# Projection matmuls of a graph layer's prologue issued ahead of their evictions, in PSUM banks of their own

## The chip, the cores and the metric

The kernel runs on one core of a Trainium2 chip. The metric is the device time of one execution in microseconds, as the median of several runs. A profiled execution has a time of its own, and the profile's "span" is the stretch of it that the trace covers.

## The reference, cut to what matters

The kernel computes one layer of a graph transformer for 6250 nodes of 256 features and 206,250 edges sorted by their target. Three parts follow each other: an attention over the edges, a linear attention over all nodes whose result is added to it, and a layer of eight experts.

```python
xn = _layernorm(x, axis=-1)
x = x + gnn(xn, edges, Wq, bq, Wk, bk, Wv, bv, Wo, bo) + linear_attention(xn, w_qkv, w_out, b_out)
x = x + experts(_layernorm(x, axis=-1), gate_w, gate_b, w1, b1, w2, b2)

# gnn: r is the source of an edge, c its target; 8 heads of 32
q = (feats @ Wq.T + bq); k = (feats @ Wk.T + bk); v = (feats @ Wv.T + bv)
sim = einsum('hed,hed->eh', q[:, c, :], k[:, r, :]) * scale
p = exp(sim - segment_max(sim, c)[c])
attn = p / segment_sum(p, c)[c]
agg = segment_sum(attn * v[:, r, :], c)
return agg @ Wo.T + bo
```

What the change touches is the first line of the attention: the layer norm of x and its products with the three weight matrices, which give the rows that the edges later gather.

## The kernel before

**Tiling.** The nodes are cut into NB = 49 blocks of P = 128 rows (the last one partly filled). D is 256, so a block's keys and values are a 128x512 tile (2 * D columns), its queries a 128x256 tile. Rows are float32 throughout.

**The prologue** writes two tables in DRAM that the rest of the kernel gathers from. `kv_tab` holds a row of keys and values for each node, `q_tab` a row of queries. It has two loops over the 49 blocks, one after the other.

The mean over features is taken out of the weights (`less_mean`, L219), so a block's matmul works on raw x, and the inverse standard deviation `rstd` is applied in the eviction. A key/value block is therefore: two matmuls over the two halves of D (L519, which the trace shows as four records, as it does for each pair of float32 matmuls) from a transposed copy of x, `xTs[k]`; one VectorE instruction (L530) that multiplies by rstd, adds the bias and writes the row buffer `kv`; one store on SyncE's queue (L533).

**x is loaded in groups** of GX = 4 blocks by `load_x` (L368): once in rows (`xg`, L383, two buffers), which ScalarE sums (`stat_sum`, L409) and squares (`stat_square`, L416) to get rstd, and once transposed (`xT`, L199, three buffers), for the matmuls. The first three groups are issued from SyncE's queue, later ones from ScalarE's own queue, where a load that has to wait for a free buffer holds up the ScalarE instructions behind it. A buffer of xT is free when the four blocks of the group that had it are through TensorE.

**Ranking of the nodes by degree** runs between the blocks of the first loop. `index_step(b)` (L501), called at the end of each block, starts gathers of pieces of the sorted edge list by GpSimd (`row_gathers`, L477; seven blocks to a set), turns them into the start of each node's edges on VectorE (`in_rows`, L488 to L492), and from block 19 on advances a generator, `rank_group` (L266), by one step a block. Its steps: two small matmuls (L271, L272), a one-hot tile (L285), six counting steps of two matmuls (L296, L298) and four VectorE instructions (L308 to L316), then three steps with VectorE one-hot tiles (`lo` L332, one buffer; `hi` L337; `rhs` L344) and up to seven matmuls each (L348).

**PSUM.** [...] The pool `bps` is a ring of five banks which `bank()` (L208) hands out in program order to whatever asks: the blocks' matmuls, the ranks' matmuls, and later all other work of the layer. The pool `qps` has three tiles of one bank each (`qc`, `pr` and `pa` of the attention loop); it exists from the start, and the prologue has no use for it.

**Order.** Each engine works through its instructions in the order of the program, and the program's order is written by hand (a manual schedule). In the first loop a block is: its two matmuls, the statistics that are due, the eviction, the store, `index_step(b)`. So the matmuls of `index_step(b)` stand between those of block b and block b+1 in TensorE's order, and the eviction of block b+1 stands behind VectorE's part of `index_step(b)`. TensorE and VectorE wait for each other by semaphores, where a tile is not ready or a buffer isn't free yet.

**Between the loops** GpSimd issues `gather_to` for the first unit of the attention: 37 gathers of 128 key/value rows each (L602, 256 KB each) into the ring `kvp` of eleven buffers. They wait for the whole of kv_tab.

**The second loop** is the same for queries: two matmuls of 256 columns a block (L616), the eviction (L620) into a row buffer `kv` of the same pool, three buffers in all, and the store to q_tab (L623); xT is loaded a second time, from ScalarE's queue. After it GpSimd gathers the query rows of the first two units (`queries`, L580), which wait for the whole of q_tab, and the attention loop begins (`units`, L1311), with the linear attention and the experts spread between its steps as background work.

Of the kernel before, what the change touches and what calls it, by code (L numbers as in the profile page):

```python
# [9 lines left out]
F32 = mybir.dt.float32  # L10
# [3 lines left out]
ALU = mybir.AluOpType  # L14
AX = mybir.AxisListType
PSUM = bass.MemoryType.PSUM
DRAM = bass.MemoryType.DRAM

P = 128
# [5 lines left out]
W = 5  # L25
# [43 lines left out]
def gps_layer(  # L69
# [34 lines left out]
    nc = tc.nc  # L104
    N, D = x.shape
    E = n_edges
    NB = -(-N // P)
# [5 lines left out]
    DC = D // P  # L113
# [18 lines left out]
    def bcast_row(ap, n, parts=P):  # L132
        return bass.AP(tensor=ap.tensor, offset=ap.offset, ap=[[0, parts], [1, n]])

    dram = ctx.enter_context(tc.tile_pool(name="dram", bufs=1, space=DRAM))
    kv_tab = dram.tile([NB * P, 2 * D], F32, name="kv_tab")
# [15 lines left out]
    with tc.manual_schedule():  # L152
# [15 lines left out]
        ident = keep.tile([P, P], F32, name="ident")  # L168
# [19 lines left out]
        rstd = keep.tile([P, NB], F32, name="rstd")  # L188
# [8 lines left out]
        def x_transposed(to, b, n=1, queue=nc.sync):  # L197

            queue.dma_start(to, xT_all[:, b * DC * P : (b + n) * DC * P])  # L199

        mctx = ExitStack()
        kvp = mctx.enter_context(tc.tile_pool(name="kvp", bufs=RING))
        cp3 = mctx.enter_context(tc.tile_pool(name="c3", bufs=3))
        cp2 = mctx.enter_context(tc.tile_pool(name="c2", bufs=2))
        qps = mctx.enter_context(tc.tile_pool(name="qps", bufs=1, space=PSUM))
        bps = mctx.enter_context(tc.tile_pool(name="bps", bufs=5, space=PSUM))

        def bank(shape):  # L208

            t = bps.tile([P, 512], F32, name="bank")  # L210
            n = math.prod(shape)
            v = t[:, :n]
            if len(shape) == 2:
                v = v.rearrange("p (a b) -> p a b", a=shape[0])
            if len(shape) == 3:
                v = v.rearrange("p (a b c) -> p a b c", a=shape[0], b=shape[1])
            return v
# [36 lines left out]
        def rank_consts(pool):  # L254
            t = {}
            t["ones_b"] = pool.tile([P, P], BF16, name="ones_b")
            nc.vector.memset(t["ones_b"], 1.0)
            t["back_b"] = pool.tile([P, P], BF16, name="back_b")
            nc.vector.tensor_scalar(t["back_b"], after, -1.0, None, op0=ALU.add)
            t["next_p"] = pool.tile([P, P], F32, name="next_p")  # L260
            nc.vector.tensor_scalar(t["next_p"], diff, -1.0, None, op0=ALU.is_equal)
            t["next_b"] = pool.tile([P, P], F32, name="next_b")
            nc.vector.tensor_scalar(t["next_b"], diff, float(P - 1), None, op0=ALU.is_equal)
            return t
# [94 lines left out]
        with ExitStack() as actx:  # L359
            ap1 = actx.enter_context(tc.tile_pool(name="a1", bufs=1))  # L360
            ap2 = actx.enter_context(tc.tile_pool(name="a2", bufs=2))
            ap3 = actx.enter_context(tc.tile_pool(name="a3", bufs=3))

            GX = 4
            NGX = -(-NB // GX)
            xgs, xTs = {}, {}

            def load_x(k, rows_too=True, queue=nc.scalar):  # L368

                if k >= NGX:  # L370
                    return
                b0 = k * GX
                n = min(GX, NB - b0)
                if rows_too:
                    xg = ap2.tile([P, GX, D], F32, name="xg")
                    xgs[k] = xg
                    full = n
                    if b0 + n == NB:
                        full = n - 1
                        nc.vector.memset(xg[:, full, :], 0.0)  # L380
                        queue.dma_start(xg[:tail, full, :], x[(NB - 1) * P : N, :])
                    if full:
                        queue.dma_start(  # L383
                            xg[:, :full, :], x[b0 * P : (b0 + full) * P, :].rearrange("(t p) d -> p t d", p=P)
                        )
                xT = ap3.tile([P, GX, DC, P], F32, name="xT")
                xTs[k] = xT
                x_transposed(xT[:, :n].rearrange("p t c q -> p (t c q)"), b0, n, queue)
# [4 lines left out]
            wn = ap1.tile([P, DC, 3 * D], F32, name="wn")  # L393
            for c in range(DC):
                nc.sync.dma_start(wn[:, c, : 2 * D], w_node[c * P : (c + 1) * P, : 2 * D])
            load_x(0, queue=nc.sync)
            bn = ap1.tile([P, 3 * D], F32, name="bn")
            nc.sync.dma_start(bn, bcast_row(b_node, 3 * D))
            load_x(1, queue=nc.sync)
            for c in range(DC):  # L400
                nc.sync.dma_start(wn[:, c, 2 * D :], w_node[c * P : (c + 1) * P, 2 * D : 3 * D])
            load_x(2, queue=nc.sync)
            rc = rank_consts(ap1)
            sums = ap1.tile([P, 2, NB], F32, name="sums")

# [5 lines left out]
            def stat_square(k):  # L411
                g = slice(k * GX, min(NB, (k + 1) * GX))
                nc.vector.tensor_scalar(sums[:, 0, g], sums[:, 0, g], -1.0 / D, None, op0=ALU.mult)
                for b in range(g.start, g.stop):
                    junk = ap1.tile([P, D], F32, name="junk")
                    nc.scalar.activation(  # L416
                        junk, xgs[k][:, b % GX, :], AF.Square, bias=sums[:, 0, b : b + 1],
                        accum_out=sums[:, 1, b : b + 1],
                    )
                nc.scalar.activation(rstd[:, g], sums[:, 1, g], AF.Sqrt, bias=eps, scale=1.0 / D)  # L420

            def stat_end(k):
                g = slice(k * GX, min(NB, (k + 1) * GX))
                nc.vector.reciprocal(rstd[:, g], rstd[:, g])
# [76 lines left out]
            def index_step(b):  # L501
# [9 lines left out]
                if b >= 8 + 5 * (need0 - 1) + 1:  # L511
                    next(ranks, None)

            stat_end(0)
            for b in range(NB):
                k = b // GX
                pkv = bank((2 * D,))
                for c in range(DC):
                    nc.tensor.matmul(  # L519
                        pkv, xTs[k][:, b % GX, c, :], wn[:, c, : 2 * D], start=(c == 0), stop=(c == DC - 1)  # L520
                    )
                if b % GX == 0 and k + 1 < NGX:
                    stat_square(k + 1)
                if b % GX == GX - 1 and k + 1 < NGX:
                    stat_end(k + 1)
                    load_x(k + 3)
                    if k + 2 < NGX:
                        stat_sum(k + 2)
                kv = ap3.tile([P, 2 * D], F32, name="kv")
                nc.vector.scalar_tensor_tensor(  # L530
                    kv, pkv, rstd[:, b : b + 1], bn[:, : 2 * D], op0=ALU.mult, op1=ALU.add
                )
                nc.sync.dma_start(kv_tab[b * P : (b + 1) * P, :], kv)  # L533
                index_step(b)
            load_x(0, False)
            load_x(1, False)
# [72 lines left out]
            sources(1)  # L609
            gather_to(len(units[0][5]))  # L610
            less_mean(wn[:, :, 2 * D :], D)
            for b in range(NB):
                k = b // GX
                pq = bank((D,))
                for c in range(DC):
                    nc.tensor.matmul(  # L616
                        pq, xTs[k][:, b % GX, c, :], wn[:, c, 2 * D :], start=(c == 0), stop=(c == DC - 1)
                    )
                q = ap3.tile([P, 2 * D], F32, name="kv")[:, :D]
                nc.vector.scalar_tensor_tensor(  # L620
                    q, pq, rstd[:, b : b + 1], bn[:, 2 * D :], op0=ALU.mult, op1=ALU.add
                )
                nc.sync.dma_start(q_tab[b * P : (b + 1) * P, :], q)  # L623
                if b % GX == GX - 1:
                    load_x(k + 3, False)
            queries(0)
            queries(1)

# [3 lines left out]
            nc.vector.tensor_reduce(bad[:, 0:1], down, AX.X, ALU.max)  # L632


        bctx = ExitStack()
        mp1 = bctx.enter_context(tc.tile_pool(name="m1", bufs=1))
        mp2 = bctx.enter_context(tc.tile_pool(name="m2", bufs=2))
# [636 lines left out]
        def weigh(v, c):  # L1274

            j0, j1 = v["chunks"][c]
            m = j1 - j0
            kv = kv_of.pop((v["u"], c))
            if c == 0:
                v["pa"] = qps.tile([P, D], F32, name="pa")  # L1280
            s0, s1 = v["s0"], v["s1"]
            vals = kv[:, :m, D:].rearrange("p j (h d) -> p j h d", d=GD)
            nc.vector.tensor_tensor(  # L1283
                vals, vals, v["pr"][:, j0 - s0 : j1 - s0, :, None].to_broadcast([P, m, GH, GD]), ALU.mult
            )
            for j in range(m):
                nc.tensor.matmul(v["pa"], ident, kv[:, j, D:], start=(j0 + j == s0), stop=(j0 + j == s1 - 1))  # L1287

        def complete(v):

# [18 lines left out]
        v = None  # L1309
        queries_of(0)  # L1310
        for u, (b, part, n_p, s0, s1, chunks) in enumerate(units):  # L1311
# [7 lines left out]
            for c in range(max(len(chunks), n_v)):  # L1319
# [5 lines left out]
                if c < len(chunks):  # L1325
                    gather_to(at + 1 + LEAD)
                    j0, j1 = chunks[c]
# [34 lines left out]
            v = new  # L1362
        for c in range(len(v["chunks"])):
            background(pace[-1] * W)
            weigh(v, c)
# [552 lines left out]
```

## Time and profile before

| What | Value |
|---|---|
| median of 3 runs | 3119.5 us (3118.4 to 3120.74) |
| the profiled execution's own time | 3534.2 us |
| its span | 3532.3 us |
| mean granted clock of TensorE | 0.812 |
| busy: TensorE matmul, VectorE, GpSimd, ScalarE | 66%, 57%, 54%, 18% of the span |
| DMA | 730.28 MB, mean 207 GB/s |
| evictions of keys and values (L530), first to last | 18.46 to 155.61 us |
| evictions of queries (L620), first to last | 158.12 to 245.20 us |
| first gather of query rows (L580) | 248.25 us |

The page and the answers of the trace give an instruction's start in us from the start of the span, its duration, its engine and line, the tiles it writes and reads, and in square brackets how long the engine had been idle before it and what ended that. "PE" is TensorE's matmul, "PEld" its weight load, "DVE" VectorE, "ACT" ScalarE, "POOL" GpSimd, "SPq" and "ACTq" the queues on which SyncE and ScalarE issue DMAs. "issue" is idle time in which the profile shows nothing that was waited for, "remote" one whose releaser it can't name. A list of waits has the waiting engine and line, what it waited for, the total, the number of times and the longest. The profiled execution is longer than an execution without the profiler, by 414.7 us here.

### The profile page before, as it was taken

To read this page: it belongs to the slowest core of one execution; us is meant where nothing else is said; L and a number is where in the kernel's file an instruction comes from. 1 tells how busy PE (TensorE), PEld (TensorE's weight loads), DVE (VectorE), ACT (ScalarE), POOL (GpSimd) and SP (SyncE) were. 2 spreads that over 40 slices of the span, in tenths; PEclk is the share of its full clock that TensorE was granted. 3 is DMA by queue.
4 is the path that set the end of the run, shared out by engine and by line. 5 is a ranking of instruction groups with operands and counts; after the bars stand their busy time and mean duration, and the time that the engine had idled before them with its cause. 6 is when DMAs were issued, how large, how long until landed. Compare 5 with 4: busy or idle time off the path is not lost.

```text
span 3532.3 us, 29535 instructions
## 1 busy us (share of the span) xinstructions
PE 2337.7 (66%) x9086; PEld 1777.0 (50%) x9086; DVE 2023.5 (57%) x2723; ACT 633.9 (18%) x1802; POOL 1920.0 (54%) x2114
## 2 busy tenths in 40 slices
PE   7844457775767643764688887743664988866395
PEld 3433335443444432553576676622543877755394
DVE  4438677776767756676565654555673655545200
ACT  4200013322323200220111111110210111111142
POOL 4243656665666656656665665566546665552101
PEclk8876678888888876896798898866876999887697
DMA  6563956655655655775777776565756887664584
GB/s 215 197 205 103 332 156 182 181 173 168 181 172 176 185 160 167 240 218 176 254 253 241 241 247 230 183 195 176 234 162 215 287 271 255 237 201 139 199 321 141
DMA packets 291643, 730.28 MB, mean 207 GB/s; under 512 B 46838, under 2 KB 152020, under 8 KB 278164
## 3 DMA queue, kind: packets, MB, share of 16 engines
q0 software_dynamic: 149744, 477.83, 44.4%
q1 hardware_dynamic: 133560, 234.37, 18.9%
q10 hardware_dynamic: 8172, 16.10, 1.5%
q8 instruction: 75, 1.23, 0.1%
q14 instruction: 92, 0.75, 0.1%
HBM read 654.47 MB, written 73.64 MB: 206 GB/s over the span
## 4 chain that ended last, share of the span: by engine, by line
PE 38%; issue 20%; DVE 15%; POOL 12%; another core or an unknown queue 6%; DMA 6%; ACT 2%; DVEq 0%; SPq 0%; POOLq 0%; ACTq 0%
PE pa L1287 13%; POOL kvg L602 10%; PE bank L1145 8%; PE bank L1162 8%; DVE kvg L1329 3%; DVE sim L1330 3%; DVE kvg L1283 3%; PE bank L709 2%; DMA kvg<-kv_tab,idx 2%; PE bank L519 2%; PE bank L866 1%; PE bank L1166 1%; PE bank L746 1%; DMA q_tab<-kv 1%
## 5 line engine op out<-in xcount | busy, mean ns | idle before, releaser
L602 POOL DMA_INDIRECT kvg<-kv_tab,idx x1715 | 1624.9, 947 | 900.7 <-issue 466.4
L1287 PE MATMUL pa<-kvg,ident 128*128 128x256 f32 x3430 | 1026.8, 454 | 646.8 <-issue 413.7
L1287 PEld LDWEIGHTS pa<-kvg,ident 128*128 128x128 f32 x3430 | 765.3, 229 | 893.2 <-issue 493.9
L1329 DVE TENSOR_TENSOR kvg<-kvg,qc 128x1280 f32<-128x1280 f32 (+1 forms) x366 | 512.3, 1400 | 334.6 <-DMA kvg<-kv_tab,idx 248.0
L1330 DVE TENSOR_REDUCE sim<-kvg 128x40 f32<-128x1280 f32 (+1 forms) x366 | 513.2, 1402 | 12.6
L1283 DVE TENSOR_TENSOR kvg<-kvg,pr 128x1280 f32<-128x1280 f32 (+1 forms) x366 | 509.5, 1393 | 0.0
L1162 PE MATMUL bank<-wt,hTe 128*128 128x256 f32 x1056 | 269.2, 396 | 44.4 <-issue 43.6
L1145 PE MATMUL bank<-xTe,wt 128*128 128x256 f32 x1056 | 271.0, 405 | 33.8 <-issue 30.3
L1145 PEld LDWEIGHTS bank<-xTe,wt 128*128 128x128 f32 x1056 | 214.3, 204 | 79.1 <-issue 45.6
L1162 PEld LDWEIGHTS bank<-wt,hTe 128*128 128x128 f32 x1056 | 207.2, 199 | 85.0 <-issue 57.2
L1303 DVE TENSOR_TENSOR ag<-pa,s 128x256 f32<-128x256 f32 x46 | 19.5, 423 | 349.8 <-PE pa L1287 242.8
L709 PE MATMUL bank<-wm,xTm 128*128 128x512 f32 x392 | 193.2, 637 | 2.5 <-issue 2.4
L801 POOL DMA_INDIRECT agg_tab<-ag,node_ri x49 | 48.5, 989 | 248.1 <-DVE ag L1303 214.2
L1226 DVE TENSOR_TENSOR res<-bank,row_b 128x256 f32<-128x256 f32 x49 | 20.6, 421 | 270.4 <-ACT bank L1222 222.3
L1151 ACT ACTIVATE hTe<-bank,wt 128x256 f32<-128x256 f32 x264 | 108.0, 474 | 374.6 <-PE bank L1145 134.5
L1205 POOL DMA_INDIRECT row_a<-ybuf,row_from x49 | 46.6, 951 | 199.3 <-issue 190.7
L746 PE MATMUL bank<-ck,cv 128*128 128x128 f32 x392 | 75.6, 340 | 97.7 <-ACT ck L738 82.0
L718 ACT ACTIVATE sq<-bank 128x512 f32<-128x512 f32 x98 | 57.0, 595 | 420.5 <-PE pa L1287 157.5
L746 PEld LDWEIGHTS bank<-ck,cv 128*128 128x128 f32 x392 | 68.2, 241 | 113.4 <-ACT ck L738 90.1
L1168 ACT COPY res<-bank 128x256 f32<-128x256 f32 x85 | 31.6, 372 | 503.1 <-issue 230.5
L709 PEld LDWEIGHTS bank<-wm,xTm 128*128 128x128 f32 x392 | 78.9, 212 | 83.8 <-issue 83.5
L726 DVE TENSOR_REDUCE rv<-sq 128x16 f32<-128x1024 f32 x49 | 59.5, 1214 | 103.2 <-ACT sq L718 71.2
(254 smaller groups left out, 2258.7 us busy)
## 6 DMA issues: line engine op xcount, KB each, us to landing
wt<-in_w_rows_dram SPq DMA_DIRECT2D x33, 1152.0 KB
wt<-in_w_rows_dram SPq DMA_DIRECT2D x33, 1028.0 KB
kvg<-kv_tab,idx POOLq DMA_INDIRECT x1715
kvg<-in_w_rows_dram SPq DMA_DIRECT2D x19, 1152.0 KB
kvg<-in_w_rows_dram SPq DMA_DIRECT2D x19, 1028.0 KB
kv_tab<-kv SPq DMA_DIRECT2D x49, 256.0 KB
in<-xbuf SPq DMA_DIRECT2D x85, 128.0 KB
ybuf<-res SPq DMA_DIRECT2D x85, 128.0 KB
```

The source lines that it names most:

```text
L519: nc.tensor.matmul(pkv, xTs[k][:, b % GX, c, :], wn[:, c, : 2 * D], start=(c == 0), stop=(c == DC - 1))
L602: nc.gpsimd.indirect_dma_start(out=kv[:, j - j0, :], out_offset=None, in_=kv_tab[:, :], in_offset=bass.IndirectOffsetOnAxis(ap=idx_of[b][: ...
L709: nc.tensor.matmul(pm, xT_of[b][:, c, :], wmf[:, c, s * MI : (s + 1) * MI], start=(c == 0), stop=(c == DC - 1),)
L726: nc.vector.tensor_reduce(rv, sqs[b], AX.X, ALU.add)
L746: nc.tensor.matmul(dots[:, hp, :], cvs[b][:, h], ckf[:, h], start=(b == 0 and hp == 0), stop=(b == NB - 1 and hp == HP - 1), skip_group_ch ...
L1145: nc.tensor.matmul(ph[:, k, :], w[:, c, f * P : (f + 1) * P], T[t]["xT"][:, c, :size], start=(k == 0 and c == 0), stop=(k == 1 and c == DC ...
L1151: nc.scalar.activation(T[t]["hT"][:, f, :size], ph[:, k, :], AF.Relu, bias=w1_t[:, V1 + f : V1 + f + 1])
L1162: nc.tensor.matmul(py, T[t]["hT"][:, f, k * P : (k + 1) * P], w[:, f, :], start=(f == 0), stop=False)
L1283: nc.vector.tensor_tensor(vals, vals, v["pr"][:, j0 - s0 : j1 - s0, :, None].to_broadcast([P, m, GH, GD]), ALU.mult)
L1287: nc.tensor.matmul(v["pa"], ident, kv[:, j, D:], start=(j0 + j == s0), stop=(j0 + j == s1 - 1))
L1329: nc.vector.tensor_tensor(keys, keys, qc[:, None, :].to_broadcast([P, j1 - j0, D]), ALU.mult)
L1330: nc.vector.tensor_reduce(sim[:, j0 - s0 : j1 - s0, :], keys.rearrange("p j (h d) -> p j h d", d=GD), AX.X, ALU.add)
```

## The change

The first loop issues the matmuls of a block two blocks ahead of its eviction, in a pool `aps` of three banks of its own; the second loop three blocks ahead. The pool takes the three banks of `qps`, which is opened only after the prologue. Row buffers are six instead of three. The rows of x go to buffers of the gather ring `kvp` instead of two of their own. All loads of x are issued on SyncE's queue, in the first loop after the store of the group's last block, in the second after the store of the group's first. In the call of `weigh` only a line break differs.

```diff
-        qps = mctx.enter_context(tc.tile_pool(name="qps", bufs=1, space=PSUM))
         bps = mctx.enter_context(tc.tile_pool(name="bps", bufs=5, space=PSUM))
...
             ap3 = actx.enter_context(tc.tile_pool(name="a3", bufs=3))
+            ap6 = actx.enter_context(tc.tile_pool(name="a6", bufs=6))
+            aps = actx.enter_context(tc.tile_pool(name="aps", bufs=3, space=PSUM))
...
-            def load_x(k, rows_too=True, queue=nc.scalar):
+            def load_x(k, rows_too=True, queue=nc.sync):
...
-                    xg = ap2.tile([P, GX, D], F32, name="xg")
+                    xg = kvp.tile([P, W, 2 * D], F32, name="kvg")[:, :GX, :D]
...
+            pkvs = {}
+
+            def keys_values(b):
+
+                if b >= NB:
+                    return
+                pkvs[b] = aps.tile([P, 2 * D], F32, name="pkv")
+                for c in range(DC):
+                    nc.tensor.matmul(
+                        pkvs[b], xTs[b // GX][:, b % GX, c, :], wn[:, c, : 2 * D], start=(c == 0), stop=(c == DC - 1)
+                    )
+
             stat_end(0)
+            keys_values(0)
+            keys_values(1)
             for b in range(NB):
                 k = b // GX
-                pkv = bank((2 * D,))
-                for c in range(DC):
-                    nc.tensor.matmul(
-                        pkv, xTs[k][:, b % GX, c, :], wn[:, c, : 2 * D], start=(c == 0), stop=(c == DC - 1)
-                    )
                 if b % GX == 0 and k + 1 < NGX:
                     stat_square(k + 1)
                 if b % GX == GX - 1 and k + 1 < NGX:
                     stat_end(k + 1)
+                kv = ap6.tile([P, 2 * D], F32, name="kv")
+                nc.vector.scalar_tensor_tensor(
+                    kv, pkvs.pop(b), rstd[:, b : b + 1], bn[:, : 2 * D], op0=ALU.mult, op1=ALU.add
+                )
+                nc.sync.dma_start(kv_tab[b * P : (b + 1) * P, :], kv)
+                if b % GX == GX - 1 and k + 1 < NGX:
                     load_x(k + 3)
                     if k + 2 < NGX:
                         stat_sum(k + 2)
-                kv = ap3.tile([P, 2 * D], F32, name="kv")
-                nc.vector.scalar_tensor_tensor(
-                    kv, pkv, rstd[:, b : b + 1], bn[:, : 2 * D], op0=ALU.mult, op1=ALU.add
-                )
-                nc.sync.dma_start(kv_tab[b * P : (b + 1) * P, :], kv)
+                keys_values(b + 2)
                 index_step(b)
             load_x(0, False)
             load_x(1, False)
...
-            for b in range(NB):
-                k = b // GX
-                pq = bank((D,))
+            pqs = {}
+
+            def query_rows(b):
+                if b >= NB:
+                    return
+                pqs[b] = aps.tile([P, 2 * D], F32, name="pkv")[:, :D]
                 for c in range(DC):
                     nc.tensor.matmul(
-                        pq, xTs[k][:, b % GX, c, :], wn[:, c, 2 * D :], start=(c == 0), stop=(c == DC - 1)
-                    )
-                q = ap3.tile([P, 2 * D], F32, name="kv")[:, :D]
+                        pqs[b], xTs[b // GX][:, b % GX, c, :], wn[:, c, 2 * D :], start=(c == 0), stop=(c == DC - 1)
+                    )
+
+            for b in range(3):
+                query_rows(b)
+            for b in range(NB):
+                q = ap6.tile([P, 2 * D], F32, name="kv")[:, :D]
                 nc.vector.scalar_tensor_tensor(
-                    q, pq, rstd[:, b : b + 1], bn[:, 2 * D :], op0=ALU.mult, op1=ALU.add
+                    q, pqs.pop(b), rstd[:, b : b + 1], bn[:, 2 * D :], op0=ALU.mult, op1=ALU.add
                 )
                 nc.sync.dma_start(q_tab[b * P : (b + 1) * P, :], q)
-                if b % GX == GX - 1:
-                    load_x(k + 3, False)
+                query_rows(b + 3)
+                if b % GX == 0 and b:
+                    load_x(b // GX + 2, False)
             queries(0)
             queries(1)
...
+        qps = mctx.enter_context(tc.tile_pool(name="qps", bufs=1, space=PSUM))
```

More of the change, by code (lines that the diff above doesn't have):

```diff
@@ L395, in gps_layer @@
                 nc.sync.dma_start(wn[:, c, : 2 * D], w_node[c * P : (c + 1) * P, : 2 * D])
-            load_x(0, queue=nc.sync)
+            load_x(0)
             bn = ap1.tile([P, 3 * D], F32, name="bn")
             nc.sync.dma_start(bn, bcast_row(b_node, 3 * D))
-            load_x(1, queue=nc.sync)
+            load_x(1)
             for c in range(DC):
                 nc.sync.dma_start(wn[:, c, 2 * D :], w_node[c * P : (c + 1) * P, 2 * D : 3 * D])
-            load_x(2, queue=nc.sync)
+            load_x(2)
             rc = rank_consts(ap1)
@@ L1286, in weigh @@
             for j in range(m):
-                nc.tensor.matmul(v["pa"], ident, kv[:, j, D:], start=(j0 + j == s0), stop=(j0 + j == s1 - 1))
+                nc.tensor.matmul(
+                    v["pa"], ident, kv[:, j, D:], start=(j0 + j == s0), stop=(j0 + j == s1 - 1),
+                )
         def complete(v):
```

## The prediction

> **What bounds the kernel now.** I read the page first, then the chain of waits, then waits and timeline of the first 250 us, since the edit touches nothing else. TensorE is busy 66% of the span, VectorE 57%, GpSimd 54%: no engine is full, and shares of the whole span say little of this stage. All later work hangs on one event, the first gather of query rows (L580), which needs every row of the query table in DRAM:
>
> ```profile
> 207.41 0.95 POOL L602 DMA_INDIRECT kvg<-kv_tab,idx  x1 [0.30 <-issue]
> 248.25 0.94 POOL L580 DMA_INDIRECT qs<-q_tab,node_ri  x1 [39.90 <-DMA q_tab<-kv]
> ```
>
> GpSimd had its 37 key/value gathers out at 208.4 and then stood idle 39.9 us for the last query row. So the prologue is one chain: keys and values of 49 blocks (evictions from 18.46 to 155.61), then queries (158.12 to 245.20). A microsecond taken from it moves the attention loop by a microsecond.
>
> Where does the first stage lose time? Waits between 13 and 157 us (engine, line, what it waited for; total, times, longest):
>
> ```profile
> ACT junk L409 <- PE bank L519: 43.7, 4, 25.0
> DVE kv L530 <- PE bank L519: 27.5, 14, 6.4
> PEld bank L519 <- DVE kv L530: 15.2, 11, 7.2
> PEld bank L348 <- DVE rhs L344: 14.1, 3, 5.4
> DVE kv L530 <- DMA kv_tab<-kv: 9.9, 6, 3.0
> DVE kv L530 <- remote: 7.6, 1, 7.6
> ```
>
> VectorE waits for TensorE and TensorE for VectorE: each holds what the other needs next. The timeline of TensorE and of VectorE shows it in the last three ranking steps:
>
> ```profile
> 98.94 3.25 PE L348 MATMUL bank<-rhs,lo 128*128 128x60 f32 x14 [4.58 <-DVE rhs L344]
> 101.97 3.14 PE L519 MATMUL bank<-wn,xT 128*128 128x512 f32 x4
> ...
> 105.15 0.75 DVE L530 SCALAR_TENSOR_TENSOR kv<-bank,rstd,bn 128x512 f32<-128x512 f32 x1 [6.19 <-PE bank L519]
> 115.45 0.75 DVE L530 SCALAR_TENSOR_TENSOR kv<-bank,rstd,bn 128x512 f32<-128x512 f32 x1 [6.21 <-issue]
> 124.40 0.75 DVE L530 SCALAR_TENSOR_TENSOR kv<-bank,rstd,bn 128x512 f32<-128x512 f32 x1 [6.44 <-PE bank L519]
> ```
>
> The ranking matmuls (L348) wait for VectorE's one-hot tiles, the next block's L519 matmuls stand behind them in TensorE's order, and the eviction waits for those: some 10 us a block. Outside ranking TensorE alone sets the pace: the chain has one piece from 120.83, 34.75 us long, "PE bank L519 x76", 1.72 us a block. In the query stage:
>
> ```profile
> DVE kv L620 <- remote: 26.8, 4, 10.7
> DVE kv L620 <- DMA q_tab<-kv: 23.5, 13, 3.4
> PEld bank L616 <- DVE kv L620: 12.2, 6, 5.6
> DVE kv L620 <- PE bank L616: 6.3, 4, 2.2
> ```
>
> Three row buffers are too few: evictions come in bursts of three and wait for a store to land. Behind the word "remote" stand stalls that no edit touches: block 11 is evicted at 50.16 though TensorE had run four blocks past it by 44.5. The profiled execution took 3534.2 us (span 3532.3), 414.7 more than the median of 3119.5. I read these stalls as part of that excess and count no gain from them; a rival takes the other view.
>
> **What the Trainium skill says.** "Perfetto Trace Analysis", Matmuls, says to rotate independent matmul groups through PSUM banks so that evictions overlap the next matmuls; the trace agrees where only L519 uses the five banks (1.72 us a block without a gap), and not where ranking takes two banks a step. "TensorE: Matmul & The Clock Gate", the HAM clock gate, says that TensorE falls to half clock after an idle window of about 3.4 us; here L519 passes stand 0.43 us apart at clock 1.00 and 0.85 apart after the long idle at 51. "DMA: Bandwidth & Descriptors", Issuing engines are not separate DMA queues, says that another issuing engine saves only the issue time; I use it for the moved loads, and no run shows it yet.
>
> **The change part by part.**
> Matmul count, evictions (0.75 and 0.48 us) and stores are unchanged; what changes is order and buffers.
>
> (1) Keys and values two blocks ahead in three banks. Blocks 0 to 19: L519 passes run at 1.72 us a block from 19.18, so block 20's matmuls would end at 19.18+19x1.72=51.9. The ranks need the third set of row gathers, whose issue GpSimd ends at 48.0 at 1.25 us each; with landing (2 us, as the stall's end at 50.1 suggests) and 1.4 us of L488 to L492 I put the eviction of block 20 at 53.5. Before it is at 69.99. Of these 16.5 us about 10 are the stall (TensorE idle 6.4 us to 50.97, then two blocks at half clock, 3.4): counted gain 6.5. Blocks 20 to 30: before 124.40-69.99=54.4 us. With matmuls ready, VectorE's own work bounds it: block 20: 0.75+1.95=2.7; six counting steps of 2.29 (80.48 to 82.77, eviction and L308 to L316): 13.7; row counting at block 23: 1.45; block 27: 3.8. Then the single buffer lo (L332) makes two steps of 3.25 (L348) plus 2.05 (lo, hi, rhs): 10.6. That is 32 up to the eviction of block 30; with 4 for hand-overs between the engines, 36. TensorE's share, ten blocks of 1.72 and 9.3 of L348, fits beside it. Gain 18. Blocks 31 to 48: banks allow two blocks ready, so 16x1.72+1=28.5 against 31.2: gain 2.7. Sum 27. Where the stall of the eviction goes, lo's single buffer is late next. I take 24, because TensorE may run steps at half clock after its idle gaps and because DMA must carry more: two stages of 128x512 rows, x and x transposed need 512 KB a block, 305 GB/s at 1.72 us; the trace shows up to 387 in a 3 us window, so it fits with little to spare. Bounds 12 to 30.
>
> (2) x through SyncE. In the first stage ScalarE's 43.7 us are cover, not cost: later it is ready in time (after the 25 us wait block 32 is evicted 1.1 us late, and TensorE never stops). Gain 0, bounds -2 to +2. On SyncE's queue each pair of loads, 1 MB, now stands ahead of the next stores: about 3 us at 340 GB/s. Six row buffers give 6x1.72=10.3 us from one use of a buffer to the next, enough for 3 us plus the 5 us that the last store took to land (156.39 to 161.3). The load waits for matmuls whose eviction is already behind it in SyncE's order: no new wait; xg in the gather ring waits for nothing. Three query loads are worse off: ScalarE issued the first at 150.21, ahead of the last evictions; on SyncE it stands behind the store of block 48. 512 KB at 340 GB/s is 1.5 us, with issue and landing about 4, before the first query matmul may start (before: 1.3 after the last eviction started). Cost 4, bounds 2 to 6; the 1.5 MB, 4.5 us, move with it.
>
> (3) Queries three ahead, six buffers. Between 163 and 188, DMA is full (0.94 to 1.03 of its time, 312 to 382 GB/s) at 1.9 us a block (eleven blocks from 164.95 to 185.69): buffers can't help; 0. After the gathers 28 blocks take 214.4 to 245.2, 1.10 each; L616 in one piece (9.76 us for 44 records, 0.89 a block) is the floor then: 26x0.21=5.5 gained. Bounds 0 to 8. Loads now come at block 4k instead of when matmuls finish: 0 to +3, I take 1. Other lines (the PSUM pool opened later, the weigh call's new line breaks) issue the same instructions: 0; their waits end before the loop.
>
> Sum: -24+4-5.5+1 = -24.5. Against the profiled execution 3534.2-24.5=3509.7, plus whatever the stalls do; against the median 3119.5-24.5=3095.
>
> **Rivals.** (A) Forecast: -15 to -35. Chance 0.62. (B) The "remote" stalls are real in every run, and a shorter prologue with six buffers loses most of them too: 10 of the key stage and, of the 27 us for three query blocks from 186 to 213, where 1.9 each would be 6, some 12, as the gathers hold the DMA until 212. -36 to -52, 3075 as its middle. For it: chain and evictions show them. Against: 414.7 us must lie somewhere in the profile alone. 0.13. (C) DMA becomes the bound in both stages: 52 MB moved until 248 us; the key stage's 26 MB (12.8 stored, 10.5 of x, 1.5 of row gathers, the rest early query loads) took 143 us, 182 GB/s; at 200 it is 130, half the gain, and the query stage gains nothing: -6 to -15, 3109. 0.11. (D) Slower: SyncE's one queue. If stores behind a 1 MB pair land over 10.3 us after their eviction, the row buffers run out once per group; beyond that point each microsecond costs ten times (ten groups). At 14 us: 10x3.7=37 lost against 24.5 gained: 3132. For it: the DMA share reaches 1.0; against: stores lead in the queue and the stage has slack while VectorE ranks. 0.07. (E) The diff's gain is absorbed, since the loop start is late for another reason (gathers end near the same time, 46 us after the table): within 6 us of before. 0.07.
>
> **How the numbers follow.** 0.2% is 6.2 us, about what a measurement here can tell from no change. Faster A+B+C=0.86, same E=0.07, slower D=0.07. The time is A's, 3095. The range leaves out B's far end and D: 3070 to 3118.
>
> **What would show it.** Right: the first qs gather moves from 248 to below 226; L530's waits of 6 us for L519 are gone; the eviction of block 30 comes some 18 us sooner after that of block 20; L620 waits less for q_tab stores after the gathers; the first L616 starts 4 to 6 us after the last L530. Wrong: L530 waits for kv_tab stores throughout, a DMA share of 1.0 in the key stage, or a loop that starts sooner and ends at the same time.

## The result, and the profile after

The changed kernel takes 3082.67 us (median of 4, 3079.39 to 3084.41) against 3120.12: ratio 0.9878, 95% interval 0.9861 to 0.9895, or 37 us less. The prediction was 3095 in a range of 3070 to 3118, faster.

The profiled execution of before that the prediction was read from, and all executions of e8, e9, e10 and a1 and of before beside them, ran at a mean TensorE clock near 0.81 and took some 3500 to 3570 us, all others near 0.85 to 0.86 and 3070 to 3130; so times are compared as ratios to the executions of before beside them, and the stages of the profile after with those of e0, the kernel before profiled again (span 3116.6 us).

Starts of the evictions and of the gathers that follow, in us, read from the timelines:

| Kernel | L530, block 20 | block 30 | block 48 | query evictions | first qs gather |
|---|---|---|---|---|---|
| before, as shown above | 70.0 | 124.4 | 155.6 | 158.1 to 245.2 | 248.2 |
| e0, before again | 59.2 | 114.9 | 146.4 | 148.7 to 223.1 | 226.2 |
| after | 55.4 | 87.2 | 118.1 | 125.0 to 183.8 | 186.8 |

From e0 to after the attention loop's start (the first gather of query rows, "qs") comes 39.3 us sooner: 28.2 in the key stage (up to the eviction of block 48) and 11.1 in the query stage (from there to the first qs gather). The two profiled spans differ by 39.0 and the medians by 37.4, so the shift is the gain and nothing of it is given back later. How far one profile can be trusted: the kernel after, e6 and e7 have the same code in the key stage, and end it at 118.1, 120.9 and 119.2.

GpSimd's lines come first: the last gather of the first unit, then the first gather of query rows, in the timeline of the kernel after. (Line numbers have moved: L602 is L615, L580 is L593, L519 is L524, L530 is L538, L348 is L347, L332 is L331, L616 is L632, L620 is L640.)

```profile
167.01 0.95 POOL L615 DMA_INDIRECT kvg<-kv_tab,idx  x1 [0.30 <-issue]
186.84 0.94 POOL L593 DMA_INDIRECT qs<-q_tab,node_ri  x1 [18.88 <-DMA q_tab<-kv]
```

The query table is still last, by 18.88 us instead of 27.06 in e0 (39.90 in the profile of before). Next come VectorE's waits between 13 and 122 us:

```profile
DVE kv L538 <- PE pkv L524: 15.8, 21, 1.0
DVE sums L415 <- ACT junk L411: 7.7, 5, 1.8
...
DVE lo L331 <- PE bank L347: 3.0, 2, 1.7
```

The eviction's longest wait for its matmuls is 1.0 us instead of 6.4: 21 short waits in the stretches where TensorE sets the pace, none in the ranking. No eviction of this stage waits for a store to kv_tab any more; in e0 they waited 16.6 us in nine. In the ranking's last steps a wait of lo for the ranking matmuls that still read it has come up, 3.0 us in two. The timelines of TensorE and of VectorE there:

```profile
77.67 3.25 PE L347 MATMUL bank<-rhs,lo 128*128 128x60 f32 x14 [3.53 <-DVE rhs L343]
80.71 3.16 PE L524 MATMUL pkv<-wn,xT 128*128 128x512 f32 x4
83.70 1.67 PE L347 MATMUL bank<-rhs,lo 128*128 128x60 f32 x14
...
77.60 0.75 DVE L538 SCALAR_TENSOR_TENSOR kv<-pkv,rstd,bn 128x512 f32<-128x512 f32 x1
80.95 1.09 DVE L331 TENSOR_TENSOR lo<-iota_f,dig 128x896 f32<-128x896 f32 x1 [1.25 <-PE bank L347]
82.94 0.75 DVE L538 SCALAR_TENSOR_TENSOR kv<-pkv,rstd,bn 128x512 f32<-128x512 f32 x1
87.18 0.75 DVE L538 SCALAR_TENSOR_TENSOR kv<-pkv,rstd,bn 128x512 f32<-128x512 f32 x1
```

The evictions of blocks 28, 29 and 30 follow VectorE's other work without a wait, 5.3 and 4.2 us apart, where e0 has 10.4 and 8.8. The second L347 group takes 1.67 us where the first took 3.25; the granted clock is 1.00 there and 0.50 in the first, which follows an idle time. Last, the waits of the query stage, 119 to 190 us:

```profile
DVE kv L640 <- DMA q_tab<-kv: 26.6, 16, 3.1
...
PE pkv L632 <- DMA xT<-in_xT_all_dram: 16.3, 8, 4.5
...
DVE kv L640 <- PE pkv L632: 14.8, 23, 5.2
```

VectorE still waits for stores to land, and TensorE now waits for x: 4.5 us at the start of the stage, and 11.8 in seven pieces after that.

### The profile page after: what moved, and what is told of

It is laid out like the page before. It is cut to its first block, busy times and chain, and to the rows that moved or that the text cites. A ratio compares the mean times of both kernels' runs of the same rounds, so it can differ in the third digit from the quotient of the medians.

```text
span 3077.6 us, 29537 instructions
## 1 busy us (share of the span) xinstructions
PE 2209.4 (72%) x9086; PEld 1722.8 (56%) x9086; DVE 2027.4 (66%) x2723; ACT 640.9 (21%) x1802; POOL 1921.5 (62%) x2114
## 3 DMA queue, kind: packets, MB, share of 16 engines
q1 hardware_dynamic: 141732, 250.47, 23.1%
## 5 line engine op out<-in xcount | busy, mean ns | idle before, releaser
L615 POOL DMA_INDIRECT kvg<-kv_tab,idx x1715 | 1625.8, 948 | 668.2 <-issue 430.1
L1309 PE MATMUL pa<-kvg,ident 128*128 128x256 f32 x3430 | 1012.1, 452 | 586.3 <-DVE kvg L1305 453.4
L1184 PE MATMUL bank<-wt,hTe 128*128 128x256 f32 x1056 | 246.9, 381 | 0.0
L1167 PE MATMUL bank<-xTe,wt 128*128 128x256 f32 x1056 | 242.6, 381 | 2.3 <-ACT xTe L1157 2.3
L1167 PEld LDWEIGHTS bank<-xTe,wt 128*128 128x128 f32 x1056 | 201.6, 191 | 30.5 <-ACT xTe L1157 3.0
L731 PE MATMUL bank<-wm,xTm 128*128 128x512 f32 x392 | 177.6, 596 | 0.0
L1190 ACT COPY res<-bank 128x256 f32<-128x256 f32 x85 | 31.7, 372 | 439.5 <-PE bank L1188 248.0
L823 POOL DMA_INDIRECT xbuf<-row_a,row_to x49 | 48.0, 980 | 95.0 <-DVE cmp L1068 66.3
L1281 ACT COPY qc<-qs 128x256 f32<-128x256 f32 x49 | 18.8, 383 | 414.5 <-DVE kvg L1353 312.5
L823 POOL DMA_INDIRECT agg_tab<-ag,node_ri x49 | 48.5, 990 | 84.2 <-DVE ag L1327 61.5
L1153 PE MATMUL bank<-ident,in 128*128 128x128 f32 x170 | 29.0, 286 | 99.9 <-DMA in<-xbuf 99.9
L760 ACT ACTIVATE ck<-bank,rk 128x64 f32<-128x64 f32 x392 | 86.1, 339 | 50.3 <-DVE rk L757 50.2
L524 PE MATMUL pkv<-wn,xT 128*128 128x512 f32 x196 | 90.9, 618 | 2.7 <-DVE kv L538 2.6
```

The source lines that it names most:

```text
L524: nc.tensor.matmul(pkvs[b], xTs[b // GX][:, b % GX, c, :], wn[:, c, : 2 * D], start=(c == 0), stop=(c == DC - 1))
L615: nc.gpsimd.indirect_dma_start(out=kv[:, j - j0, :], out_offset=None, in_=kv_tab[:, :], in_offset=bass.IndirectOffsetOnAxis(ap=idx_of[b][: ...
L731: nc.tensor.matmul(pm, xT_of[b][:, c, :], wmf[:, c, s * MI : (s + 1) * MI], start=(c == 0), stop=(c == DC - 1),)
L760: nc.scalar.activation(cks[b][:, h, :], pms[b][0][:, h * MD : (h + 1) * MD], AF.Copy, scale=rk[:, h : h + 1])
L823: s = nc.gpsimd.indirect_dma_start(**kw)
L1167: nc.tensor.matmul(ph[:, k, :], w[:, c, f * P : (f + 1) * P], T[t]["xT"][:, c, :size], start=(k == 0 and c == 0), stop=(k == 1 and c == DC ...
```

## Experiments

**e0: the kernel before, once more.** No edit.

> The kernel before, profiled once more. Theory (the remote stalls belong to one profiled execution): a span near 3118, no eviction (L530, L620) that waits over 5 us for remote, last L530 near 146, first qs gather near 224 (186.8 of the kernel after plus the 37.4 us that the medians differ by). Rival (the stalls are in every execution): a span near 3530 under the profiler again, or a span of 3120 with the first qs gather still near 248.

Measured: 3118.46 us, span 3116.6, last L530 at 146.4, first qs gather at 226.2. No eviction waits for "remote"; VectorE's waits up to 230 us begin:

```profile
DVE kv L620 <- DMA q_tab<-kv: 47.3, 26, 4.4
...
DVE kv L530 <- PE bank L519: 34.3, 14, 6.4
DVE kv L530 <- DMA kv_tab<-kv: 16.6, 9, 3.3
```

The 6.4 us waits for L519 are here too, and the waits for q_tab stores are twice those of the profile above, where stalls stood in their place. Rival B falls: the stalls are no part of the 3120 us against which the change was timed.

**e1: one part alone, the look-ahead.** To the kernel before:

```diff
-                pkv = bank((2 * D,))
-                (the two matmuls of block b)
+                (pkvs.pop(b), filled two blocks ahead from a pool of three banks)
...
                 nc.sync.dma_start(kv_tab[b * P : (b + 1) * P, :], kv)
+                keys_values(b + 2)
                 index_step(b)
```

> The kernel before plus one part of the change: the key/value matmuls two blocks ahead in three banks of their own. Three row buffers, x on ScalarE's queue and the query loop stay. Theory (TensorE's order in the ranking steps): 20 to 25 us less than before, about 3097, L530 to L530 of blocks 20 to 30 near 34 us. Rival (row buffers and the query loop bring it): at most 8 us less, 3112 or more.

Measured: 3100.13 us, ratio 0.9912 (0.9893 to 0.9932), some 24 us less than before beside it. The key stage ends at 127.0 and the first qs gather is at 206.8, 19.3 and 19.4 sooner than in e0 (the profiled spans differ by 17.9, less than the medians; why is open). The whole of it comes in the ranking: blocks 20 to 30 take 32.4 us instead of 55.7. So the theory holds for the ranking steps, and the query stage, untouched, is as long as in e0 (79.7 us). Outside the ranking the look-ahead alone gains nothing: block 20 is evicted at 61.5, 2.3 later than in e0, and blocks 30 to 48 take 33.2 us instead of 31.5. With three row buffers the evictions (L539 here) still wait for stores, between 13 and 128 us:

```profile
DVE kv L539 <- DMA kv_tab<-kv: 20.4, 12, 3.2
```

The 8.9 us of the key stage that e1 lacks against the kernel after need another part of the change; e3 says which.

**e2: the change without the first loop's look-ahead.**

```diff
+                keys_values(b)
                 if b % GX == 0 and k + 1 < NGX:
...
-                keys_values(b + 2)
                 index_step(b)
```

> The kernel after with the look-ahead of the first loop taken out: each block's key/value matmuls directly ahead of its eviction, still in three banks of their own; six row buffers, SyncE's loads and the new query loop stay. Theory (the order of TensorE's instructions): 18 to 25 us more than the kernel after, about 3104. Rival (banks apart from the ranks' are enough): within 5 us of the kernel after.

Measured: 3109.09 us, ratio 0.9946 (0.993 to 0.9963), against 0.9878 for the change; the key stage ends at 143.2 instead of 118.1. Nothing else differs between the two. Banks of its own do not help a matmul that stands behind the ranking's in TensorE's order. The timeline has the old picture back:

```profile
92.70 0.75 DVE L537 SCALAR_TENSOR_TENSOR kv<-pkv,rstd,bn 128x512 f32<-128x512 f32 x1 [6.27 <-PE pkv L524]
103.04 0.75 DVE L537 SCALAR_TENSOR_TENSOR kv<-pkv,rstd,bn 128x512 f32<-128x512 f32 x1 [6.25 <-PE pkv L524]
111.96 0.75 DVE L537 SCALAR_TENSOR_TENSOR kv<-pkv,rstd,bn 128x512 f32<-128x512 f32 x1 [6.41 <-PE pkv L524]
```

**e3: the change with three row buffers.**

```diff
-            ap6 = actx.enter_context(tc.tile_pool(name="a6", bufs=6))
+            ap6 = actx.enter_context(tc.tile_pool(name="a6", bufs=3))
```

> The kernel after with three row buffers instead of six. Theory (first loop by order, query loop by row buffers and DMA): 8 to 14 us more than the kernel after, about 3093, nearly all of it in the query loop. Rival (DMA is full in the query loop, buffers do nothing): within 3 us of the kernel after.

Measured: 3109.63 us, ratio 0.9948 (0.9931 to 0.9964): more lost than expected. The key stage ends 7.8 us later than in the kernel after: its evictions wait 23.1 us in eleven pieces for stores to kv_tab, where the kernel after has no such wait. So the rest of the key stage's gain hangs on the row buffers. The query stage takes 88.2 us instead of 68.7, which is longer than in e0 and e1, although the matmuls have a lead. Loads of x ahead of the stores on one queue may cost more than the lead brings; no run has three buffers and the other queue, so this is not shown. The waits of 126 to 215 us:

```profile
DVE kv L640 <- DMA q_tab<-kv: 49.9, 31, 4.4
...
PEld pkv L632 <- DVE kv L640: 32.1, 23, 4.2
```

Two views of the 45 us in which GpSimd issues the gathers show why buffers help where I had called DMA full. The columns are: from, to, length, busy time of TensorE, its weight load, VectorE, ScalarE and GpSimd, each with its count, granted clock, DMA share, GB/s. First e3, then the kernel after:

```profile
130.00:175.00 45.00, 30.12 (x98) 21.54 (x99) 10.64 (x22) 0.00 (x0) 34.03 (x37) 0.84 0.97 331
```

```profile
123.00:168.00 45.00, 33.14 (x133) 25.40 (x134) 14.51 (x32) 0.00 (x0) 34.04 (x36) 0.96 1.01 372
```

VectorE evicts 22 blocks in the one and 32 in the other. The DMA share hardly tells the two apart, and the rate rises only from 331 to 372 GB/s. But the 37 gathers of 256 KB are 9.7 MB in both, 215 GB/s over 45 us; by this estimate 116 GB/s are left for the query rows and their x with three buffers and 157 with six, a third more. A store takes longer to land (median 5.3 us against 3.7), but twice as many can be under way.

**e4: loads of x on ScalarE's queue again.**

```diff
-            def load_x(k, rows_too=True, queue=nc.sync):
+            def load_x(k, rows_too=True, queue=nc.scalar):
```

(The first three loads stay on SyncE's.)

> The kernel after with the loads of x back on ScalarE's queue (from the fourth group on), at the same places in the program. Theory (the queue itself is worth little; ScalarE gets the first query loads out while SyncE still stores): first qs gather 0 to 5 us sooner than the 186.8 of the kernel after, time 0 to 5 us less, near 3080. Rival (ScalarE held up by loads was part of the loss): statistics late, evictions of the first loop wait for L415, 5 us more or worse.

Measured: 3078.24 us, ratio 0.9857 (0.9834 to 0.988); the interval meets that of the change. The key stage ends 3.9 us later, the stage after it is 2.5 shorter (66.2 against 68.7): first qs gather 188.2, 1.3 later than in the kernel after where 0 to 5 sooner were expected. The queue by itself is worth nothing that these runs can tell. ScalarE still waits 17.5 us for L524 in the key stage, without effect on the end.

**e5: query loads sooner.** Four buffers for transposed x (five row buffers, for room); the first three groups of the query loop are loaded after blocks 39, 43 and 47 of the key loop, the others one group sooner.

```diff
+                if b % GX == GX - 1 and k >= 9:
+                    load_x(k - 9, False)
                 keys_values(b + 2)
...
-                    load_x(b // GX + 2, False)
+                    load_x(b // GX + 3, False)
```

> The kernel after with four buffers for transposed x, five row buffers, and the query loop's first three groups of x loaded from the end of the first loop, the later ones one group sooner. Theory (TensorE's waits for x in the query loop, 4.5 us at its start and 11.8 later, lie on the path): first qs gather 4 to 10 us sooner than 186.8, time 4 to 10 us less than the kernel after. Rival (DMA is full there, so a sooner load only moves the wait): within 2 us, or a little slower from the fifth buffer's lack.

Measured: 3081.61 us, ratio 0.9865 (0.9842 to 0.9888), no difference that the intervals show; first qs gather at 181.7, 5.1 sooner, of which 3.9 are the query stage's. The first query matmul starts 1.3 us after the last key eviction, nearly as in e0 (1.2), instead of 5.3. TensorE's waits for x are gone, its waits for VectorE (12.5 and 18.1 us for matmuls and weights) stand in their place, and VectorE waits for stores as before (27.1): of the waits for x, little more than the late start was on the path. (One row buffer less may hide a gain; that was not run alone.)

**e6: fewer gathers ahead of the query loop.**

```diff
-            gather_to(len(units[0][5]))
+            gather_to(LEAD + 1)
```

> The kernel after with three chunks (about 14 gathers) ahead of the query loop instead of all 37 of the first unit; the others follow in the attention loop. Theory (the query loop is bound by DMA bytes and the loop's start by the query table): 23 gathers or 5.9 MB less at 400 GB/s, the first qs gather 10 to 15 us sooner, but GpSimd then owes 23x1.25=29 us of gathers to the loop, so that the time is within 8 us of the kernel after. Rival (the time follows the first qs gather alone): 10 to 15 us less.

Measured: 3074.09 us, ratio 0.9835 (0.9809 to 0.9861). First qs gather at 182.0, 4.9 sooner where 10 to 15 were expected; the query stage is 7.7 shorter, as this profile's key stage ended later on the same code. Once the gathers are out, at 140.7, TensorE is the floor of the query loop: from 145 to 175 it is busy 4.3 to 5.0 of every 5 us, with DMA at 225 to 321 GB/s. The gain in time, some 13 us by the ratios, is larger than either; whether GpSimd's later gathers help the attention loop or this is the intervals' width is open.

**e7: no loads of x in the query loop.** It leaves out the x of blocks 12 to 48 and takes that of the first three groups again.

```diff
-                        pqs[b], xTs[b // GX][:, b % GX, c, :], wn[:, c, 2 * D :], ...
+                        pqs[b], xTs[(b // GX) % 3][:, b % GX, c, :], wn[:, c, 2 * D :], ...
...
-                if b % GX == 0 and b:
-                    load_x(b // GX + 2, False)
```

> The kernel after without the query loop's loads of x beyond its first three groups: blocks from 12 on are computed from the x of those groups, so the query rows are another matter, with the same instructions but ten loads (4.9 MB) fewer. Theory (DMA bytes bound the query loop while the gathers run): the loop's last eviction near 171 instead of 183.8 and 10 to 14 us less in all. Rival (row buffers and the landing of stores bound it, whatever else DMA carries): last eviction within 4 us of 183.8.

Measured: 3070.6 us, ratio 0.9832 (0.981 to 0.9855). The last query eviction is at 172.6, 11.1 sooner than in the kernel after; in the 45 us of the gathers 46 blocks are evicted instead of 32. The view from 160 to 165 us:

```profile
160.00:165.00 5.00, 5.00 (x24) 4.20 (x23) 2.54 (x6) 0.00 (x0) 3.77 (x5) 1.00 1.01 353
```

TensorE is busy for all of it, and DMA's share is 1.01 at only 353 GB/s. In the kernel after, then, the ten loads of x are worth 11 us of this stage. e7 takes away TensorE's waits for them together with their bytes; e5 takes away the waits and leaves the bytes of these ten loads, and shortens the query stage by 3.9 us, the late start's size. So it is the bytes that bind while the gathers run, as far as e5 with its five row buffers can tell.

**e9, e10: row buffers alone, and with the look-ahead.** To the kernel before, and to e1:

```diff
-                    xg = ap2.tile([P, GX, D], F32, name="xg")
+                    xg = kvp.tile([P, W, 2 * D], F32, name="kvg")[:, :GX, :D]
...
-                kv = ap3.tile([P, 2 * D], F32, name="kv")
+                kv = ap6.tile([P, 2 * D], F32, name="kv")
...
-                q = ap3.tile([P, 2 * D], F32, name="kv")[:, :D]
+                q = ap6.tile([P, 2 * D], F32, name="kv")[:, :D]
```

> The kernel before with six row buffers instead of three, the room for them made by putting the rows of x into the gather ring as the change does. Order of matmuls, banks and queues stay as before. Theory (the row buffers work on their own, in the query loop while the gathers fill DMA): last L530 within 3 us of the 146.4 of the kernel before, last L530 to first qs gather 66 to 70 us instead of 79.8, time 10 to 16 us less than before. Rival (buffers help only once TensorE runs ahead in banks of its own): less than 5 us.

> The kernel before with two parts of the change: the first loop's look-ahead in its own banks, and six row buffers (rows of x in the gather ring). Loads stay on ScalarE's queue and the query loop keeps the five-bank ring and its old order. Theory (these two parts are the whole gain): first qs gather at 188 to 193, time within 5 us of the kernel after. Rival (the query loop's own banks and three blocks of lead matter): 8 us or more behind the kernel after.

Measured beside a before of 3556.54 us: e9 3546.86, ratio 0.9975 (0.9947 to 1.0003), 10 us less by the medians but not clear of none, so that neither theory nor rival is decided; e10 3532.67, ratio 0.9932 (0.9911 to 0.9953). The kernel after beside them, **a1**:

> The kernel after once more, beside the others on the same chip. All theories: 3080 to 3086, the first qs gather at 185 to 190.

Measured: 3534.77 us, ratio 0.9941 (0.9922 to 0.996). All these profiles have stalls that the expectations did not reckon with: evictions of query rows wait 37.6 us for "remote" in e9 and in e10, and 18.9 in a1. The last L530 of e9 is at 149.4, but its query stage is 87.5 us long and not 66 to 70; the first qs gather is at 223.3 in e10 and 232.0 in a1. What e9's buffers do shows in the waits for q_tab stores: 2.3 us in three, against 23.5 in thirteen in the profile of before with its stalls. As ratios, e10 and a1 are the same: here look-ahead and row buffers are the whole gain, within intervals of 0.2% to either side. Whether moving the loads and giving the query loop banks and a lead of its own add something where there are no stalls was not run; e3 against e1, 88.2 us of query stage against 79.7, says that with three buffers they do not.

**e8: a version with more.** e5 and e6 together, and two query rows' tiles in each row buffer:

```diff
-                q = ap6.tile([P, 2 * D], F32, name="kv")[:, :D]
+                if b % 2 == 0:
+                    pair = ap6.tile([P, 2 * D], F32, name="kv")
+                q = pair[:, b % 2 * D : (b % 2 + 1) * D]
```

> The kernel after with three more edits: four buffers for transposed x and sooner query loads (five row buffers), two query rows' tiles in each row buffer (ten query rows), and three chunks of gathers ahead of the query loop. Theory (query loop bound by DMA bytes, by x at its start and by row buffers while gathers run): first qs gather at 166 to 175, 8 to 16 us less than the kernel after, near 3070. Rival (the attention loop's start is held by the gathers it now owes): within 5 us of the kernel after.

Measured: 3509.35 us, ratio 0.9886 (0.9848 to 0.9924), against a1's 0.9941: 25 us by the medians, more than expected; it beats both kernels here, though its interval just meets a1's. Its first qs gather is at 195.9 against a1's 232.0; its parts e5 and e6 gave 0.9865 and 0.9835 against 0.9878 where executions are shorter; the sum was not run there.

## Why the prediction was right, point by point

**The base.** The prediction left about 10 us of the key stage uncounted, as belonging to that execution, which puts the end of that stage before the change at about 146. e0 has 146.4 and no stall. That the excess of 414.7 us lies in the profiler is wrong, though: executions of e9's and a1's group took as long without it. What makes them long is open.

**(1) Look-ahead: the mechanism is right, the closeness of the end is luck.** The end was put at 53.5+36+28.5=118.0 and is at 118.1, but the three terms miss by 1.9, -4.3 and 2.5 and cancel. Block 20 is at 55.4. From block 20 to 30 the sum of VectorE's own work was 32, to which 4 were added for hand-overs: the runs give 31.7, so the 4 do not show; with the matmul ready, an eviction follows the instruction before it at once. From 30 to 48 two blocks were to be ready ahead; TensorE takes 1.72 us for each of the 18, 31.0 in all, where e0 takes 31.5.

Against e0 the three gains are 3.7, 24.0 and 0.5, together 28.2, where 6.5, 18 and 2.7 were counted and 24 of the sum taken. Nor is all of it the look-ahead's: by itself it brings 19.3 (e1), and in the first twenty blocks nothing. The Trainium skill, "Perfetto Trace Analysis", Matmuls, asks for matmul groups to rotate through banks so that evictions overlap; e2 qualifies that: with three banks to rotate through and no lead in the program's order, the key stage ends at 143.2.

**(2) x through SyncE: right in its price, but what was called cover is part of the gain.** The late start was priced at 4; from last key eviction to first query matmul it is 5.3 us instead of 1.2, and e5, which takes it away, shortens the query stage by 3.9. The 0 for ScalarE's 43.7 us is borne out by e4's time. That stores behind a load need more than three buffers was given only as cover. e3, with three, loses 7.8 us in the key stage, which the sum had put down to the look-ahead, and 19.5 in the query stage.

**(3) Query loop: the step that was mis-sized.** "DMA is full (0.94 to 1.03 of its time, 312 to 382 GB/s)... buffers can't help; 0" is wrong. In 45 us of the gathers 21 blocks are evicted in e0, 22 in e3 and 32 in the kernel after, and the rate rises from 331 (e3) to 372 GB/s. After the gathers, 5.5 were counted from 0.21 a block; a block takes 0.95 us instead of e0's 1.03, and 17 are left instead of 23. With the late start and the loads the query stage was to be 0.5 shorter, and is 11.1. This and the 4.2 that (1) took too little are 14.8 us of shift, and 13 in time, by which the forecast fell short.

**The rivals.** A: the 37 us lie outside A's own 15 to 35, inside the stated range. B: its 36 to 52 hold the number, but not for its reason, as e0 shows; and where the stalls are in the timed executions, the change brings 22 us (a1), with stalls left. C: the key stage of the kernel after moves 25.4 MB at 240 GB/s, above the 200 assumed; DMA does bind the query stage while the gathers run (e7), but at 383 to 408 GB/s (140 to 170). D: no eviction of the key stage waits for a kv_tab store; e3 shows that the mechanism is real once buffers run out. E: no absorption, 39.3 us of shift against 37 in time. Of the signs, a first qs gather below 226 was a weak one: e0, without the change, has 226.2.

## What to carry to other kernels

Where two engines hold each other up, look at the order of instructions on the engine: give the producer a lead in the program, not only banks of its own (the kernel after and e2 differ in just this, 118.1 against 143.2). A lead needs buffers behind it too: with three row buffers a third of the key stage's gain was missing (e1). A DMA share near 1.0 doesn't say that no more bytes would fit: before calling a stage full, look for the highest GB/s that any stretch reaches, and count how many transfers the buffers allow at once. When a wait is to be removed, add up the waiting engine's own work from durations first; here that sum was better than the sum with allowances.

## What the runs showed of the hardware

While the gathers ran, stretches of 5 us had a DMA share of 1.04 at 383 to 408 GB/s in the kernel after (140 to 170), of 1.00 to 1.05 at only 346 to 363 in e7 (145 to 170), and of 0.93 at 299 in e3 (150 to 155): the share does not rank stretches by the bytes they move. The median time of a query store to land was 3.1 and 3.7 us with three row buffers (e0, e3) and 5.3 with six (after), at mean rates of the stage of 284, 259 and 336 GB/s.

The Trainium skill, "TensorE: Matmul & The Clock Gate", Part 1: The HAM clock gate, gives an idle window of about 3.4 us before half clock. In the kernel after, an idle time of 3.53 us was followed by a granted clock of 0.50 and an L347 group of 3.25 us, against 1.67 at clock 1.00 where TensorE had gone on working. But in e0 an idle time of 2.61 us, shorter than that window, was enough: the clock of the next 2.5 us was 0.53, and twelve ranking matmuls took 2.71 us, against 1.55 in the kernel after at 1.00. The measurement decides: a shorter idle time can do it.
